# Hidden rows of an FP4 feed-forward layer as three tiles of columns, and the last ten token tiles turned on TensorE

## The chip, the cores and the metric

The kernel runs on one core of one Trainium2 chip. The metric is the device time of one execution in microseconds; a median over runs is given. A second number, the span, is the time from the first to the last instruction in one profiled execution.

## The reference

A transformer layer over 8 sequences of 1024 tokens with 512 features, all in float32. First latent attention on the normalised input, then a feed-forward block whose weights and activations are rounded to a 4-bit grid in blocks of 16, each with a residual:

```python
x = x + attn(layernorm(x))               # 16 heads of 32 + 16 rotary columns, latent 128, causal
x = x + ffn(layernorm(x))

def fp4_quant_dequant(x):                # blocks of 16 along the last dimension
    scale = max(abs(xb)) / 6, at least 1e-12
    return nearest(GRID, abs(xb / scale)) * sign(xb) * scale     # GRID 0 .5 1 1.5 2 3 4 6

def ffn(x):                              # 512 -> 1408 -> 512
    gate = q(x) @ q(w_gate).T
    up   = q(x) @ q(w_up).T
    h    = silu(gate) * up
    return q(h) @ q(w_down).T
```

Here `q` is `fp4_quant_dequant`. What matters below is that a row of `h`, 1408 values of one token, is quantised along the row, and then has to stand with its 1408 values along the partitions, because TensorE sums over partitions. A tile of 128 tokens by 1408 columns has to be turned between the up and the down product.

## The kernel before

The 8192 tokens are 64 token tiles of 128 rows, numbered n; four of them, 512 tokens, form a unit, and a sequence is two units. A unit's attention is made of score steps: scores on TensorE, exponentials on ScalarE (L612), the clip and the sums on VectorE (L627, L656) and GpSimd (L630, L634), then the product with the values. A first unit of a sequence has 3 steps for each of four groups of heads, a second unit 7. The output projection (`out_proj`, L770) of a unit runs early in the next one; `fetch_wo` (L764) loads its weights again each time, and the result is stored to DRAM as `mid`, from which the feed-forward part reads it again as `y` and, for the residual, as `xr`.

The feed-forward work of earlier units is cut into pieces (`ffn_pieces`, L904) and laid between the score steps of later ones as fillers, so that TensorE has work while exponentials are computed. For token tile n the order is: `gate(n, 0..2)`, then `down(n - 2)`, then `up(n, 0..2)`; columns 0 to 511, 512 to 1023 and 1024 to 1407 are the three parts k (`FCH`, L31). Between them, `begin(n + 1)` puts the normalisation and quantisation of the next y in the VectorE order, `turned(n + 1)` turns it on TensorE, and `fetch(n + 2)` loads the one after it.

- `gate` multiplies and ScalarE copies the sum out of PSUM into the row tile `h` (L836, recorded at L142). `h` has two buffers, so the row of tile n uses the memory of tile n - 2, and the copy has to wait until that row has been moved away.
- `up` multiplies and VectorE forms the product with the gate in place (L851). After the last part the whole row of 1408 is put in VectorE's list: one maximum for the whole row (L261), the scales (L266 to L271), then for each part six passes that round it (L288, L296, L299, L302 twice, L284) and a transposition of its 32 x 32 blocks (L311).
- When all three parts are turned, `hidden_turned` (L862) sends 16 DMAs (`move_blocks`, L229, the issue is at L237) that carry the blocks to their places in `hT`. There is one buffer of `hT`; the move of tile n is sent after `down(n - 1)` has used its own. Each DMA carries 32 partitions with 11 runs of 32 values.
- `down` waits for the move, and TensorE runs the product of 11 chunks into one PSUM bank; VectorE adds the residual (L899), and the store to `out` is sent (L902).
- The last token tile alone (`BY_PE`, L250) is turned on TensorE inside `down`: 11 transposes by the identity (`turn`, L215) into PSUM, and ScalarE copies them into `hT`.

Three PSUM banks (`bank`, L212) serve all products except scores and values, in turn: a product can start when the bank of the third last one has been read.

The order on TensorE, VectorE and ScalarE is written out by the program itself while it is built. A class `Clock` keeps an estimated time for each of the three. `slack` and `quantize` put VectorE jobs with estimated costs into two queues; `on_dve` fills the time up to a job's estimated readiness with jobs from the queues (`fill`); `need(key)` lays all jobs up to a key at once, before the piece that needs them. DMAs that wait for a moment (`send`, `pass_on`, `sent_by_now`) are put in SyncE's queue when TensorE's estimated time passes that moment or when something asks for them. All loads, stores and moves of the main part go through that one queue of SyncE, which works in order: an issue that waits holds all behind it. `MOVE` (L249) is the estimated time of a move.

The moves of the normalised x of the attention part (`xnT`, also 16 DMAs for 256 rows of tokens, twice per unit) use the same function and the same queue.

In the first four units, in place of feed-forward pieces, `weight_pieces` (L322) loads the feed-forward weights in chunks, quantises them with the same jobs and turns them on TensorE; the chunks lie in the two buffers of `h` and that of `hT`.

Of the kernel before, what the change touches and what calls it, by code (L numbers as in the profile page):

```python
# [42 lines left out]
def tile_mla_then_fp4_ffn(  # L43
# [149 lines left out]
    pair = p1.tile([P, 2, D], F32, tag="xp", name="xp_0_0")  # L193
    for t in range(2):
        nc.sync.dma_start(out=pair[:, t, :], in_=x[0, t * P : (t + 1) * P, :])
    other = p1.tile([P, NFC, P], F32, tag="hT", name="x_0").rearrange("p n k -> p (n k)")
    for t in range(2):
        nc.sync.dma_start(out=other[:, t * D : (t + 1) * D], in_=x[0, (2 + t) * P : (3 + t) * P, :])
    first_x = [pair[:, t, :] for t in range(2)] + [other[:, t * D : (t + 1) * D] for t in range(2)]
    nc.scalar.dma_start(out=wdkv, in_=w_dkv.rearrange("(c p) n -> p c n", p=P))  # L200
    nc.scalar.dma_start(out=wdq, in_=w_dq.rearrange("(c p) n -> p c n", p=P))
    nc.scalar.dma_start(out=wkr, in_=w_kr.rearrange("(c p) n -> p c n", p=P)[:, :, 32:64])
# [43 lines left out]
        clk.sent_by_now(key)  # L246
        clk.pe = max(clk.pe, arrive.pop(key))

    MOVE = 9.0  # L249
    BY_PE = (4 * 2 * B - 1,)  # L250


    def quantize_jobs(q, width, key, scales_in):

        nb = width // BLK
        q3 = q.rearrange("p (b k) -> p b k", k=BLK)
        got, jobs = {}, []

        def amax():
            got["sc"], got["rs"] = sc, rs = scales_in()  # L260
            nc.vector.tensor_reduce(rs, q3, AX.X, ALU.max, apply_absolute_value=True)  # L261

        def scales():
            sc, rs = got["sc"], got["rs"]

            nc.vector.tensor_scalar(sc, rs, 1.0 / 6.0, None, ALU.mult)  # L266
            nc.vector.scalar_tensor_tensor(rs, sc, -4.0, rs, ALU.mult, ALU.add)
            nc.vector.scalar_tensor_tensor(rs, sc, -2.0, rs, ALU.mult, ALU.add)
            nc.vector.scalar_tensor_tensor(sc, rs, 1.0 / 6.0, sc, ALU.mult, ALU.add)
            nc.vector.tensor_scalar(sc, sc, 1e-12, None, ALU.max)  # L270
            nc.vector.reciprocal(rs, sc)  # L271

        jobs.append((0.06 + 0.0011 * width, amax, key, True))
        jobs.append((1.1 + 0.008 * nb, scales, key, True))
        for o in range(0, width, 512):
            step = min(512, width - o)
            part, bl = q[:, o : o + step], slice(o // BLK, (o + step) // BLK)
            nbl = step // BLK
            part3 = part.rearrange("p (b k) -> p b k", k=BLK)

            def times(which, part3=part3, bl=bl, nbl=nbl):
                by = got[which][:, bl].unsqueeze(2).to_broadcast([P, nbl, BLK])
                if which == "sc":
                    nc.vector.tensor_tensor(part3, part3, by, ALU.mult)  # L284
                else:


                    nc.vector.scalar_tensor_tensor(  # L288
                        part3, part3, BELOW_ONE, by, ALU.mult, ALU.mult
                    )  # L290

            def steps(part=part, step=step):
                got["m"] = m = p1.tile([P, 512], F32, tag="m", name="m")[:, :step]
                nc.vector.tensor_scalar(  # L296
                    m.bitcast(U32), part.bitcast(U32), EXP_MASK, None, ALU.bitwise_and
                )
                nc.vector.tensor_scalar(m, m, 1.0, MAGIC, ALU.max, ALU.mult)  # L299

            def to_grid(op, part=part):
                nc.vector.tensor_tensor(part, part, got["m"], op)  # L302

            pass_cost = 0.06 + 0.00125 * step
            jobs.append((pass_cost, lambda f=times: f("rs"), key, True))
            jobs.append((1.2 * pass_cost, steps, key, True))
            jobs.append((pass_cost, lambda f=to_grid: f(ALU.add), key, False))
            jobs.append((pass_cost, lambda f=to_grid: f(ALU.subtract), key, False))
            jobs.append((pass_cost, lambda f=times: f("sc"), key, True))
            if key[0] == "h" and key[1] not in BY_PE:  # L310
                jobs.append((0.72, lambda p=part: nc.vector.transpose(p, p), key, True))  # L311
        return jobs

    def quantize(q, width, key):
        def own():
            return [p1.tile([P, 88], F32, tag=x, name=x)[:, : width // BLK] for x in ("sc", "rs")]

        for cost, run, k, free in quantize_jobs(q, width, key, own):
            clk.later.append((cost, run, k, 0.0, free))


    def weight_pieces():  # L322
# [4 lines left out]
            chunks.append([(w_gate[rows, :], wg_T[:, :, rows]), (w_up[rows, :], wu_T[:, :, rows])])  # L327
        for c in range(NDC):
            rows = slice(c * P, (c + 1) * P)
            chunks.append([(w_down[rows, :], wd_T[:, :, rows])])  # L330
        raws = {}

        def load(i):

            if i % 3 < 2:
                raw = p2.tile([P, FF], F32, tag="h", name="wraw")
            else:
                raw = p1.tile([P, NFC, P], F32, tag="hT", name="wraw_hT")
                raw = raw.rearrange("p n k -> p (n k)")
            raws[i], at = raw, 0  # L340
            for src, _ in chunks[i]:
                nc.sync.dma_start(out=raw[:, at : at + src.shape[1]], in_=src)
                at += src.shape[1]
            quantize(raw[:, :at], at, ("w", i))

        def piece(i, at, dst, off, n):
            if i == 0 and at == 0:
                for k in range(3):
                    load(k)
            clk.need(("w", i))  # L350
            turn(raws[i][:, at : at + n * P], dst[:, off : off + n], n)
            if at + n * P == sum(src.shape[1] for src, _ in chunks[i]):
                raws.pop(i)
                if i + 3 < len(chunks):
                    load(i + 3)

        pieces = []
        for i, parts in enumerate(chunks):
            at = 0
            for src, dst in parts:  # L360
                for off, width in FCH if src.shape[1] == FF else [(0, D)]:
                    n = width // P
                    pieces.append((i, at, dst, off // P if src.shape[1] == FF else 0, n))
                    at += width
        return [(0.5, lambda x=x: piece(*x)) for x in pieces]


# [435 lines left out]
    def begin(n):  # L803
# [1 line left out]
        yTs[n] = yT = p2.tile([P, NDC, P], F32, tag="yT", name="yT")  # L805
        jobs = normed(ys[n], ("y", n))
        scales_in = lambda: (yT[:, 0, : D // BLK], yT[:, 1, : D // BLK])
        jobs += [x[:3] for x in quantize_jobs(ys[n], D, ("y", n), scales_in)]
        ahead_of_rows(jobs)

    def hidden(n, w, off, width):
# [9 lines left out]
        return pg  # L821

    def turned(n):
        clk.need(("y", n))
        clk.pe = max(clk.pe, clk.dve)
        yT = yTs.pop(n)
        turn(ys[n], yT, NDC)
        ys[n] = yT

    def gate(n, k):  # L830
        if k == 0:
            clk.need(("h", n - 2))
            clk.sent_by_now(("h", n - 2))
            hs[n] = p2.tile([P, FF], F32, tag="h", name="h")
        off, width = FCH[k]
        copy_out(hs[n][:, off : off + width], hidden(n, wg_T, off, width))  # L836
        if k == 2:
            silus.append(
                lambda: on_act(4.0, lambda: nc.scalar.activation(hs[n], hs[n], AF.Silu))
            )  # L840

    def up(n, k):
        while silus:
            silus.popleft()()
        off, width = FCH[k]
        h = hs[n][:, off : off + width]
        pg = hidden(n, wu_T, off, width)
        on_dve(
            0.1 + 0.00115 * width,
# [2 lines left out]
        )  # L852
        if k == 2:
            ys.pop(n)
            quantize(hs[n], FF, ("h", n))
            slack(0.0, lambda: hidden_turned(n), ("h", n))

    hTs = {}

    waits, used = {}, set()  # L860

    def hidden_turned(n, done=None):  # L862

        if n in BY_PE:
            return
        if n > 0 and n - 1 not in used:
            waits[n] = clk.dve
            return
        h = hs.pop(n)

        def make():
            hTs[n] = p1.tile([P, NFC, P], F32, tag="hT", name="hT")
            return hTs[n]

        move_blocks(h, make, ("h", n), clk.dve if n == 0 or done is None else max(done, clk.pe))

    def down(n):
        clk.need(("h", n))
        clk.sent_by_now("store")
        ends[n] = p3.tile([P, D], F32, tag="xo", name=f"xr_{n}")  # L880
        nc.sync.dma_start(out=ends[n], in_=mids.pop(tiles[n]))
        if n in BY_PE:
            hTs[n] = p1.tile([P, NFC, P], F32, tag="hT", name="hT")
            for off, width in FCH:
                f0, c = off // P, width // P
                turn(hs[n][:, off : off + width], hTs[n][:, f0 : f0 + c, :], c)
            hs.pop(n)
        else:
            arrived(("h", n))
        hT = hTs[n]  # L890
        pd = bank("pd")
        for i in range(NFC):
            mm(pd, lhsT=hT[:, i, :], rhs=wd_T[:, i, :], start=(i == 0), stop=(i == NFC - 1))
        hTs.pop(n)
        used.add(n)
        if n + 1 in waits:
            hidden_turned(n + 1, waits.pop(n + 1))
        xt = ends.pop(n)
        on_dve(0.7, clk.pe + 0.3, lambda: nc.vector.tensor_tensor(xt, pd, xt, ALU.add))  # L899
        u, t = tiles[n]  # L900
# [161 lines left out]
```

## Time and profile before

| what | value |
|---|---|
| median of three runs | 3772.24 us (3765.41 to 3773.14) |
| the profiled execution | 3769.9 us |
| its span | 3768.2 us |
| TensorE's granted clock, mean | 0.976 |
| TensorE busy | 3550.3 us (94%) |
| VectorE busy | 2852.6 us (76%) |
| ScalarE busy | 1136.8 us (30%) |
| GpSimd busy | 669.8 us (18%) |
| DMAs for hT, xnT on SyncE's queue | 1008, 480 |

An engine is busy while one of its instructions runs; the rest of the span it is idle, and a list of waits names what ended each idle time. "ACT h L142 <- DMA hT<-h" reads: ScalarE, about to write `h` at line 142, was idle until the DMA that moves `h` into `hT` had landed. Tile names leave buffer numbers out. A timeline line gives the start in us from the span's beginning, the length, the engine, the line, the operation, the tiles written and read with their shapes, and how many were merged in the line. A row of stretches gives, for each, its length, the busy time and number of instructions of TensorE, its weight loads, VectorE, ScalarE and GpSimd, then the granted clock, the share of the DMA engines and GB/s. An issue on SyncE's queue is a sequencer's work, not counted as busy; its length is the time that the queue was taken by it.

### The profile page before, as it was taken

The numbers are of one execution on the slowest core, as the hardware profiler recorded it, in microseconds if no ns is written. First come the engines' busy times: TensorE is split into PE (matmuls) and PEld (weight loads), VectorE is DVE, ScalarE is ACT, GpSimd is POOL, SyncE is SP. The second block draws the span as 40 slices with busy tenths as digits, with TensorE's granted clock in tenths as the row PEclk, the third lists the DMA queues.
The fourth block names the chain that finished last, engine by engine and source line by source line (L and its number), as shares of the span: only waits on it lengthen the run. The fifth ranks groups of instructions, "written<-read, shape, count | busy, mean of one in ns | idle before, by whom it ended". The sixth has DMA issues, their size and how long they took to land.

```text
span 3768.2 us, 45975 instructions
## 1 busy us (share of the span) xinstructions
PE 3550.3 (94%) x17119; PEld 1550.3 (41%) x17119; DVE 2852.6 (76%) x5024; ACT 1136.8 (30%) x1473; POOL 669.8 (18%) x838
## 2 busy tenths in 40 slices
PE   6997989999999999999999999999999999998998
PEld 3333334443444444444444444444443444443343
DVE  4886856787868778877888687887877886777876
ACT  2443442332223233223233332233323322332210
POOL 1333331111111111211111111112111111111100
PEclk9998999999999999999999999999999999999999
DMA  3212211222122211223121222212122112211122
GB/s 83 70 35 70 72 34 45 55 50 44 33 69 44 74 40 37 47 62 76 34 44 33 67 50 66 44 33 72 43 68 44 33 33 75 52 39 33 42 63 39
DMA packets 577038, 192.47 MB, mean 51 GB/s; under 512 B 514864, under 2 KB 515888, under 8 KB 576816
## 3 DMA queue, kind: packets, MB, share of 16 engines
q1 hardware_dynamic: 568512, 187.36, 21.1%
q10 hardware_dynamic: 8304, 2.18, 0.3%
q8 instruction: 136, 2.23, 0.2%
q14 instruction: 86, 0.70, 0.1%
HBM read 94.72 MB, written 33.55 MB: 34 GB/s over the span
## 4 chain that ended last, share of the span: by engine, by line
PE 58%; DVE 14%; SPq 6%; issue 3%; DMA 2%; ACT 2%; POOL 1%; DVEq 0%; ACTq 0%; POOLq 0%
PE pg L129 21%; PE pd L129 11%; PE sc_ps L129 8%; SPq L237 6%; PE po L129 5%; PE num L129 4%; PE pp L129 2%; DVE h L302 2%; DVE pT L656 2%; PE den L129 1%; DVE h L311 1%; DVE h L284 1%; DMA hT<-h 1%; PE pv L129 1%; PE pqr L129 1%
## 5 line engine op out<-in xcount | busy, mean ns | idle before, releaser
L612 ACT ACTIVATE pT<-sc_ps 128x1024 f32<-128x1024 f32 (+1 forms) x640 | 567.3, 940 | 1137.4 <-PE sc_ps L129 1020.0
L129 PE MATMUL pg<-wg_T,yT 128*128 128x512 f32 (+1 forms) x1536 | 641.7, 569 | 2.4 <-ACT h L142 1.7
L129 PE MATMUL pg<-wu_T,yT 128*128 128x512 f32 (+1 forms) x1536 | 638.9, 562 | 0.0
L129 PE MATMUL pd<-wd_T,hT 128*128 128x512 f32 x1408 | 620.8, 597 | 8.1 <-ACT h L142 5.3
L630 POOL TENSOR_SCALAR pT<-pT 128x1024 f32<-128x1024 f32 (+1 forms) x320 | 351.3, 1098 | 1049.1 <-ACT pT L612 677.4
L634 POOL TENSOR_SCALAR_AFFINE_SELECT pT<-pT 128x256 f32<-128x256 f32 (+1 forms) x384 | 238.9, 622 | 1587.9 <-DVE pT L627 1410.2
L656 DVE TENSOR_TENSOR pT<-pT 128x1024 f32<-128x1024 f32 (+3 forms) x528 | 463.7, 904 | 3.7 <-POOL pT L634 0.6
L627 DVE TENSOR_SCALAR pT<-pT 128x1024 f32<-128x1024 f32 (+1 forms) x320 | 206.2, 644 | 327.7 <-ACT pT L612 326.9
L129 PEld LDWEIGHTS pg<-wg_T,yT 128*128 128x128 f32 x1536 | 294.4, 194 | 337.4 <-issue 256.0
L129 PEld LDWEIGHTS pg<-wu_T,yT 128*128 128x128 f32 x1536 | 282.6, 190 | 315.7 <-issue 248.7
L129 PEld LDWEIGHTS pd<-wd_T,hT 128*128 128x128 f32 x1408 | 265.0, 190 | 349.7 <-issue 327.2
L129 PE MATMUL sc_ps<-qc,kT 32*128 32x512 f32 (+3 forms) x3072 | 342.4, 530 | 25.0 <-ACT pT L612 24.9
L142 ACT COPY h<-pg 128x512 f32<-128x512 f32 (+1 forms) x192 | 102.4, 554 | 786.5 <-DMA hT<-h 415.0
L129 PE MATMUL num<-pT,v 128*32 128x512 f32 (+3 forms) x3072 | 327.8, 499 | 11.8 <-POOL pT L634 11.2
L129 PE MATMUL sc_ps<-qr,kr 32*128 32x512 f32 (+3 forms) x3072 | 309.2, 487 | 4.2 <-DVE qr L548 4.2
L129 PE MATMUL po<-wo,aT 128*128 128x512 f32 x512 | 236.5, 622 | 36.6 <-DMA wo<-in_w_o_dram 24.5
L302 DVE TENSOR_TENSOR h<-h,m 128x512 f32<-128x512 f32 (+1 forms) x384 | 260.1, 677 | 10.7
L851 DVE TENSOR_TENSOR h<-pg,h 128x512 f32<-128x512 f32 (+1 forms) x192 | 122.6, 639 | 127.9 <-PE pg L129 124.3
L129 PEld LDWEIGHTS sc_ps<-qc,kT 32*128 32x128 f32 x3072 | 115.5, 185 | 242.1 <-issue 149.8
L129 PEld LDWEIGHTS sc_ps<-qr,kr 32*128 32x128 f32 x3072 | 146.8, 188 | 109.7 <-issue 84.2
L129 PEld LDWEIGHTS po<-wo,aT 128*128 128x128 f32 x512 | 101.5, 200 | 169.2 <-issue 121.8
L129 PEld LDWEIGHTS num<-pT,v 128*32 128x32 f32 x3072 | 67.9, 108 | 224.8 <-issue 132.3
(109 smaller groups left out, 3412.7 us busy)
## 6 DMA issues: line engine op xcount, KB each, us to landing
hT<-h SPq DMA_DIRECT2D x1008, 44.0 KB, 2.1
xo<-in_x_dram SPq DMA_DIRECT2D x64, 256.0 KB, 2.7
wo<-in_w_o_dram SPq DMA_DIRECT2D x16, 1024.0 KB, 5.2
mid<-xo SPq DMA_DIRECT2D x64, 256.0 KB, 2.2
y<-mid SPq DMA_DIRECT2D x64, 256.0 KB, 2.8
xr<-mid SPq DMA_DIRECT2D x64, 256.0 KB, 2.7
out_dram<-xr SPq DMA_DIRECT2D x64, 256.0 KB, 2.0
xp<-in_x_dram SPq DMA_DIRECT2D x30, 512.0 KB, 3.9
```

The source lines that it names most:

```text
L129: nc.tensor.matmul(dst, **kw)
L142: on_act(0.1 + 0.0009 * src.free_size(), lambda: nc.scalar.copy(dst, src))
L237: nc.sync.dma_start(out=dst[32 * q : 32 * q + 32, :, 32 * g : 32 * g + 32], in_=src4[32 * g : 32 * g + 32, q],)
L284: nc.vector.tensor_tensor(part3, part3, by, ALU.mult)
L302: nc.vector.tensor_tensor(part, part, got["m"], op)
L311: jobs.append((0.72, lambda p=part: nc.vector.transpose(p, p), key, True))
L612: lambda: nc.scalar.activation(part, sc[:, 2 * k : 2 * k + 2, :cols], AF.Exp, scale=SM_SCALE),
L627: lambda: nc.vector.tensor_scalar(part, part, E_HI, E_LO, ALU.min, ALU.max),
L630: nc.gpsimd.tensor_scalar(part, part, E_HI, E_LO, ALU.min, ALU.max)
L634: nc.gpsimd.affine_select(out=diag, in_=diag, pattern=[[0, 2], [0, len(segs)], [1, P]], compare_op=ALU.is_ge, fill=0.0, base=0, channel_mu ...
L656: lambda a=whole, b=part: nc.vector.tensor_tensor(a, a, b, ALU.add),
L851: lambda: nc.vector.tensor_tensor(h, pg, h, ALU.mult),
```

## The change

The row of a token tile is no longer one tile of 1408 columns but three (512, 512 and 384), with tags h0, h1, h2 and two buffers each; `hT` likewise becomes hT0, hT1, hT2 with one buffer each. What follows from that in the code:

- `quantize_jobs` takes a list of parts. The maximum is one reduction per part; the scales are still computed once for the row. The jobs of part k have the key (name, n, k), so that a piece can ask for one part.
- After the transposition of a part on VectorE, `row_turned(n, k)` sends the 16 DMAs of that part, or leaves it waiting until `down(n - 1)` has used its part k. A row is moved by 48 DMAs instead of 16, each with 4 or 3 runs of 32 values per partition instead of 11.
- `gate(n, k)` asks for part k of tile n - 2 instead of the whole row, and `down` waits for a part ahead of that part's matmuls.
- `BY_PE` holds the last ten token tiles, 54 to 63. Their rows are not turned on VectorE and not moved; `turn_here` turns part k on TensorE just ahead of `gate(n + 2, k)`, or inside `down` for the last two.
- Silu runs once for each part, one after the other. The weights are loaded, quantised and turned in such parts too, and w_down comes in three DMAs per chunk.
- `MOVE` is 8.0 instead of 9.0, and some estimated costs of the planner differ.

```diff
-    MOVE = 9.0
-    BY_PE = (4 * 2 * B - 1,)
+    MOVE = 8.0
+    BY_PE = range(4 * 2 * B - 10, 4 * 2 * B)
...
-        def amax():
-            got["sc"], got["rs"] = sc, rs = scales_in()
-            nc.vector.tensor_reduce(rs, q3, AX.X, ALU.max, apply_absolute_value=True)
+        def amax(part, at):
+            if at == 0:
+                got["sc"], got["rs"] = scales_in()
+            nc.vector.tensor_reduce(
+                got["rs"][:, at : at + part.shape[1] // BLK],
+                part.rearrange("p (b k) -> p b k", k=BLK),
...
-            if key[0] == "h" and key[1] not in BY_PE:
-                jobs.append((0.72, lambda p=part: nc.vector.transpose(p, p), key, True))
+            if then is not None:
+                jobs.append((1.0 * cost, lambda p=part, k=k: then(p, k), name, True))
...
     def gate(n, k):
-        if k == 0:
-            clk.need(("h", n - 2))
-            clk.sent_by_now(("h", n - 2))
-            hs[n] = p2.tile([P, FF], F32, tag="h", name="h")
         off, width = FCH[k]
-        copy_out(hs[n][:, off : off + width], hidden(n, wg_T, off, width))
+        if n > 1:
+            clk.need(("h", n - 2, k))
+            if n - 2 in BY_PE:
+                turn_here(n - 2, k)
+            clk.sent_by_now(("h", n - 2, k))
+        hs[n, k] = p2.tile([P, width], F32, tag=f"h{k}", name=f"h{k}")
+        copy_out(hs[n, k], hidden(n, wg_T, off, width))
...
+    def row_turned(n, k, done=None):
+
+        if done is None:
+            done = clk.dve
+        if n > 0 and (n - 1, k) not in used:
+            waiting[n, k] = done
+            return
+        h = hs.pop((n, k))
+
+        def make():
+            hTs[n, k] = p1.tile([P, FCH[k][1] // P, P], F32, tag=f"hT{k}", name="hT")
+            return hTs[n, k]
+
+        move_blocks(h, make, ("h", n, k), max(done, clk.pe if (n, k) in waiting else done))
+
+    def turn_here(n, k):
+        width = FCH[k][1]
+        clk.pe = max(clk.pe, clk.dve)
+        hTs[n, k] = p1.tile([P, width // P, P], F32, tag=f"hT{k}", name="hT")
+        turn(hs.pop((n, k)), hTs[n, k], width // P)
...
     def down(n):
-        clk.need(("h", n))
...
+        for k, (off, width) in enumerate(FCH):
+            if n in BY_PE:
+                if (n, k) not in hTs:
+                    clk.need(("h", n, k))
+                    turn_here(n, k)
+            else:
+                arrived(("h", n, k))
+            for i in range(off // P, (off + width) // P):
+                mm(
+                    pd,
+                    lhsT=hTs[n, k][:, i - off // P, :],
...
+            hTs.pop((n, k))
+            used.add((n, k))
+            if (n + 1, k) in waiting:
+                row_turned(n + 1, k, waiting[n + 1, k])
+                waiting.pop((n + 1, k))
```

## The prediction

> **What bounds the kernel now.** The page's busy row comes first: no other engine is near TensorE. Lines marked L are the kernel's; PE is TensorE, ACT ScalarE, DVE VectorE, SPq the queue of SyncE.
>
> ```profile
> span 3768.2 us, 45975 instructions
> PE 3550.3 (94%) x17119; PEld 1550.3 (41%) x17119; DVE 2852.6 (76%) x5024; ACT 1136.8 (30%) x1473; POOL 669.8 (18%) x838
> ```
>
> So the change can win only what is left of TensorE's idle 218 us, and lose by lengthening it. The list of waits says who the idle time is for; a row gives the total in us, how often, and the longest.
>
> ```profile
> ACT h L142 <- DMA hT<-h: 415.0, 31, 25.9
> PE pqr L129 <- ACT h L142: 41.9, 5, 9.0
> PE pp L129 <- ACT h L142: 13.5, 5, 3.1
> DVE ny L376 <- DMA y<-mid: 38.5, 16, 4.8
> ```
>
> ScalarE's copy of a new gate row waits 31 times until the row two tiles earlier, which has the same buffer, has been moved. Mostly that is hidden; ten times TensorE then waits for a PSUM bank. The timeline around one of the five long ones (start, length, engine, and in brackets the idle time before it):
>
> ```profile
> 1366.43 1.06 PE L129 MATMUL num<-pT,v 128*32 128x512 f32 x8
> 1375.82 2.08 PE L129 MATMUL pqr<-cq,wqr 128*128 128x512 f32 x2 [8.32 <-ACT h L142]
> ...
> 1375.18 0.59 ACT L142 COPY h<-pg 128x512 f32<-128x512 f32 x1 [17.82 <-DMA hT<-h]
> ...
> 1362.98 10.51 SPq L237 DMA_DIRECT2D hT<-h  x16
> ```
>
> The move is 16 issues in a row on SyncE's queue, 10.5 us, and lands 1.4 us later; only then may the copy write. Cut into stretches from tile 15's gate on, the profile repeats every 10 tiles, with some 18 us of TensorE idle in each:
>
> ```profile
> 1359.00:1868.00 509.00, 491.20 (x2213) 215.59 (x2212) 397.76 (x703) 152.43 (x194) 85.36 (x106) 0.98 0.22 51
> 1868.00:2377.00 509.00, 489.23 (x2201) 214.54 (x2200) 394.51 (x699) 151.07 (x191) 83.06 (x104) 0.98 0.22 50
> ```
>
> **What the change can win.** A part of a row is moved when VectorE has turned it, and a gate copy waits for its own part alone. Tile 14's parts are turned by 1341.7, 1357.3 and 1362.9. Its first move can run 1341.7 to 1352.2, so the copy at 1362.7 need not wait, and the 8.32 us go. The same holds for the second idle stretch of the period, 2.59 us ahead of a pp matmul at 1470.0 (tile 16's parts are turned by 1438.6, 1452.0, 1457.0; copies at 1461 and 1465). After a gap TensorE also runs slower for a while: behind the long one the pqr pair takes 2.08 us instead of 1.12 and the next 16 gate matmuls 7.86 instead of 7.03, together 1.8; behind the short one the pp group takes 3.56 instead of 1.99, 1.6. The Trainium skill (TensorE: Matmul & The Clock Gate, "HAM oscillation — how this bites in real kernels") asks only that there be no idle gap above about 3.4 us; by that the short gap would cost nothing after itself, and the sum would be 5 x 1.6 = 8 us less gain. I take the row. Per period 8.3 + 1.8 + 2.6 + 1.6 = 14.3; five periods: 71.5. In the start-up of this stretch one gap of 1.7 (662.8) goes: 2.
>
> At the end (from 3333): gaps of 2.05, 0.81, 7.77 and 6.69, behind copies that waited 15 to 18.5 us for moves, 17.3, and about 5 of slow clock: 22. From 3600 on, five gaps ahead of down matmuls (1.16, 1.56, 1.99, 0.57, 2.86): 8. The last tile's second product starts with the part that is ready instead of after all three: the last matmuls now end at 3763.8; turning part by part they end about 5 earlier.
>
> The price there: nine more tiles are turned on TensorE, 99 transposes. Those of y are 256 in 39.3 us, so 0.153 each: 15, all of it on the bounding engine. Taken away with it: 9 x (0.71 + 0.71 + 0.57) = 18 us of VectorE's transposes and 144 DMAs. The 27 copies out of PSUM (0.59) fall to ScalarE, 30% busy. If that cover fails they cost 16. The maximum as three reductions costs VectorE 2 x 0.685 + about 0.53 against 1.61, 0.3 a tile, 19 in all, which balances the 18; three Silu calls for one cost ScalarE some 0.3 a tile. The weight loads keep their pace: each is turned 512 columns at a time as before. Sum of the gains: 71.5 + 2 + 22 + 8 + 5 - 15 = 93.
>
> **What it costs on SyncE's queue.** A move of a part is still 16 DMAs, so 54 tiles issue 48 each instead of 16: 2592 for 1008. Does a DMA of 128 pieces (4 column blocks) cost less to issue than one of 352 (11)? The trace has two sizes, 352 pieces for hT and 256 for xnT; the columns are least/median/most ns.
>
> ```profile
> L237 SPq DMA_DIRECT2D hT<-h x1008: 585/616/1884, 651.0 to 3735.1; - x168
> ...
> L237 SPq DMA_DIRECT2D xnT<-xp x480: 585/609/1823, 70.3 to 3199.7; - x160
> ```
>
> Same floor, medians 7 ns apart: the price is per DMA. With the 44 ns between, 16 take 10.5 us, three parts 31.5, of a mean 50.9 us per tile. The Trainium skill speaks against such a price: DMA: Bandwidth & Descriptors, "Anatomy of one DMA — SWDGE (gpsimd) path", puts sequencer dispatch at about 50 ns and most of the 2 us in the landing. With that, 48 DMAs would hold the queue for 2.4 us and nothing below would be late. But that section tells of GpSimd's path, and the row is this queue: I take 0.6. Ends: 0.24 a DMA if it fell with the pieces (a part 3.8 us, no loss), 0.66 if not.
>
> The queue is in order, and what stands behind a row's moves now comes up to 21 us later, less the time between its first and last part (5 to 25). Two things stand there.
>
> First, **the output projection's weights**. Once in a period:
>
> ```profile
> 1579.57 10.50 SPq L237 DMA_DIRECT2D hT<-h  x16
> 1590.12 0.60 SPq L189 DMA_DIRECT2D xo<-in_x_dram  x1
> 1590.84 0.39 SPq L768 DMA_DIRECT2D wo<-in_w_o_dram  x1
> ...
> 1596.71 15.37 PE L129 MATMUL po<-wo,aT 128*128 128x512 f32 x32 [3.57 <-DVE h L851]
> ```
>
> wo lands at 1596.6 and po starts at 1596.7: no slack. Tile 19's parts are turned at 1570.9, 1575.3 and 1579.4; three moves from 1570.9 end at 1602.4, wo is issued near 1603, 12.4 later. At the five such places I get 11.2, 12.4, 11.9, 12.4 and 11.3: 59 us, straight onto TensorE, whose matmuls behind po (scores too) wait with it.
>
> Second, **y and xo**, which VectorE reads in order. At 1319.19 y is issued right behind tile 13's move (parts turned 1297.7, 1302.6, 1308.5). Three moves from 1297.7 end at 1329.2, y lands 2.9 after its issue, at 1332.6; its statistics (L376) stand at 1323.4: VectorE waits 9 us, and behind L376 wait the clips, the up products and the bank releases. VectorE is busy 397 of 509 us, so some is absorbed. I pushed each lateness down VectorE's order, let its idle gaps eat it, and took as a TensorE stall what exceeds the distance from an instruction's end to the matmul that needs it (median 9.4 us for the clips, 5.0 for the up products' banks, 4.4 for the down sums). The 20 y loads that stand directly behind a move: 76 us of stalls; xo: 19; all y loads, if the parts overtake those too: 160, with xo 180. Floor 0: a VectorE delay could be made up wholly. I take 76 + 19 = 95, since only those 20 are sure to be behind.
>
> Other effects: the part that a copy waits for is now the third. By the same queue arithmetic third copies wait 5.5, 7.5 and some 8.3 us three times a period, just before the 9.7 us of down matmuls that hide them: 0. xnT has 12 us of slack or more when it follows one part: 0, up to 7 a period if it follows two.
>
> **Sum.** The profiled run took 3769.9 us (span 3768.2), inside the three runs shown (median 3772.2). 3769.9 - 93 + 59 + 95 = 3831; I say 3830, 1.5% slower.
>
> **Rivals.** (1) *The queue's delay is absorbed on VectorE.* For it: 22% idle. Only wo bites: 3770 - 93 + 59 = 3736, faster. (2) *Small DMAs are cheaper to issue.* Against it, the equal floors. It decides the sign: at about 9 us a part the same pushing gives 50 instead of 180, and wo about 40; then the sum is 3740 to 3770, and below 7 us a part near 3680. (3) *All y loads are late*, VectorE becomes the bound in the odd blocks: 3770 - 93 + 59 + 180 = 3916. (4) *The parts don't come early*: a part's jobs are forced only at its own gate, behind the next y's jobs (about 7 us), so moves start late and copies still wait. For it: half of the tiles are finished within 5 us of their gate now. Gains fall to 30, losses too, near 3800. (5) Gains and losses cancel, 3763 to 3777.
>
> **How the numbers follow.** Forecast 0.43 (its own range 3785 to 3880); (1) 0.17; (2) 0.12; (3) 0.12; (4) 0.09; (5) 0.07. Faster is (1) and (2), 0.29; within 0.2%, about what a measurement can tell, 0.07; slower the rest, 0.64. The range leaves out the cheapest half of (2), and the worst part of (3): 3690 to 3915.
>
> **What would show it.** Right: hT issues of 2592 at 585 ns or more, SPq near 55% busy; the ACT wait for hT well below 415 us and the pqr gap gone; waits of po for wo grown by 11 to 12 us in five places; the y wait above 38.5 us, many times over. Wrong: issues near 300 ns; wo overtaking the moves because the planner sends parts later; y waits that stay small; or stalls of TensorE on turned parts after tile 54.

## The result, and the profile after

| what | before | after |
|---|---|---|
| median | 3771.01 us | 4149.17 us (4146.40 to 4150.56) |
| span of the profiled execution | 3768.2 us | 4148.5 us |
| TensorE busy, idle | 3550, 218 us | 3654, 495 us |
| mean granted clock | 0.976 | 0.944 |
| gaps of TensorE over 1.5 us | 41, together 177 us | 71, together 437 us |

The changed kernel is slower by 10.0%: ratio 1.1004, 95% interval 1.0985 to 1.1023. The forecast was 1.5%. Of the 380 us more in the span, 277 are idle time of TensorE. The other 103 are longer busy time: 15 for the 99 transposes, by the 0.153 us of the prediction, and 88 left over, at a lower clock: the granted clock stood at 0.50 for 184 us of the run before and for 471 us of this one.

The head of the page after the change:

```profile
span 4148.5 us, 49052 instructions
...
PE 3653.5 (88%) x17218; PEld 1584.8 (38%) x17218; DVE 2848.9 (69%) x5144; ACT 1168.4 (28%) x1628; POOL 662.1 (16%) x838
```

VectorE has as many busy microseconds as before (2848.9 against 2852.6), so no work was added to it that could matter. It waits more. The list of waits of the changed kernel (total us, times, longest), the first two over all engines, the rest TensorE's own:

```profile
DVE ny L386 <- DMA y<-mid: 470.0, 47, 23.1
...
ACT h L142 <- DMA hT<-h: 240.8, 46, 11.9
...
PE pg L129 <- DVE xr L931: 129.8, 20, 8.8
PE po L129 <- DMA wo<-in_w_o_dram: 90.0, 7, 15.9
PE num L129 <- DVE pT L637: 64.4, 24, 8.2
PE num L129 <- POOL pT L644: 59.6, 33, 6.2
PE pv L129 <- DVE xr L931: 36.1, 5, 7.7
```

The wait that was to be shortened, ScalarE's for the move, fell from 415.0 to 240.8 us and from 25.9 at the longest to 11.9. The rows of TensorE waiting for that copy (41.9 and 13.5 us before) are gone from its list. In their place VectorE's wait for y rose from 38.5 us in 16 places to 470.0 in 47. TensorE pays for it at many places: a product that waits for a bank which VectorE's residual sum (L931) has yet to read, and values that wait for clipped exponentials (L637, and L644 on GpSimd behind it).

One such case shows the whole path. SyncE's queue, then VectorE, then TensorE, each a timeline of the changed kernel (start, length, engine, line, operation, idle time ahead of it in brackets):

```profile
1973.40 10.24 SPq L237 DMA_DIRECT2D hT<-h  x16
...
1984.39 21.18 SPq L237 DMA_DIRECT2D hT<-h  x32
2005.67 0.53 SPq L811 DMA_DIRECT2D y<-mid  x1
```

```profile
1995.99 0.69 DVE L311 TENSOR_TENSOR h<-h,m 128x512 f32<-128x512 f32 x1
2008.50 0.69 DVE L386 BATCH_NORM_STATS2 ny<-y 128x6 f32<-128x512 f32 x1 [11.82 <-DMA y<-mid]
...
2024.04 0.71 DVE L876 STREAM_TRANSPOSE h<-h 128x512 f32<-128x512 f32 x1
...
2026.38 0.68 DVE L931 TENSOR_TENSOR xr<-pd,xr 128x512 f32<-128x512 f32 x1
```

```profile
2018.97 1.99 PE L129 MATMUL pp<-xnT,wdkv 128*128 128x256 f32 x8
2027.12 9.37 PE L129 MATMUL pg<-wu_T,yT 128*128 128x512 f32 x16 [6.15 <-DVE xr L931]
```

The load of y stands behind two parts of a move, 32 issues. It goes out at 2005.67 and has landed by 2008.5. VectorE stands at its statistics for 11.82 us, and behind them in its order stand the sum that frees a bank and the rest of the row that it had begun to round. TensorE idles 6.15 us for the bank and then runs its 16 matmuls in 9.37 instead of 7.03, with the granted clock at 0.50 up to 2031.66. The row's first part is turned only at 2024.04, so its own move starts late as well. Such lateness could feed on itself, if the next y stood behind that move. Here it does not: the next y goes out at 2041.80, when its buffer has just become free. But the head of SyncE's queue does wait longer for a transposed part than it did; the kernel before, then the changed one:

```profile
SPq L237 <- DVE h L311: 218.8, 55, 12.2
```

```profile
SPq L237 <- DVE h L876: 623.9, 42, 31.3
```

While the head of the queue waits for VectorE, all loads behind it wait too. Nearly all of the 623.9 us are waits for the first part of a row, 42 of them, 15 us in the mean: the queue has come to the move long before VectorE has turned the part. How much of the rise comes of late loads of y is seen in the first experiment below. From the end of the transposes that free y's buffer to the issue of the next y, over tiles 3 to 53, the mean was 2.5 us before and is 13.2 now (medians 0.6 and 13.5). Of these 51 loads 43 went out more than 1 us late, where 21 did before, and 36 more than 10 us late, where none did. Those that directly follow an hT move rose from 15 to 31. Ten tiles took 509 us; now they take 587. From tile 54 on, where no rows are moved, this vanishes. Stretches of 50 us (length; busy time and count of TensorE, its loads, VectorE, ScalarE, GpSimd; clock, DMA share, GB/s), one from the main part and one from the end:

```profile
1700.00:1750.00 50.00, 35.45 (x149) 15.77 (x142) 16.88 (x31) 9.02 (x13) 7.71 (x10) 0.86 0.40 108
...
4000.00:4050.00 50.00, 50.00 (x141) 24.29 (x140) 41.27 (x87) 9.13 (x18) 1.09 (x2) 1.00 0.05 16
```

Without moves TensorE has no gap in these 50 us and runs at full clock. The stretch of the main part has one of the five long waits for wo, 14.55 us at a mean clock of 0.86, and is worse than most: from tile 0's gate to tile 54's, 394 of 3154 us are idle, where the kernel before has 101 of 2756.

### The profile page after: what moved, and what is told of

Same layout as the page of the kernel before. It is cut to its first block, busy times and chain, and to the rows that moved or that the text cites. A ratio compares the mean times of both kernels' runs of the same rounds, so it can differ in the third digit from the quotient of the medians.

```text
span 4148.5 us, 49052 instructions
## 1 busy us (share of the span) xinstructions
PE 3653.5 (88%) x17218; PEld 1584.8 (38%) x17218; DVE 2848.9 (69%) x5144; ACT 1168.4 (28%) x1628; POOL 662.1 (16%) x838
## 5 line engine op out<-in xcount | busy, mean ns | idle before, releaser
L622 ACT ACTIVATE pT<-sc_ps 128x1024 f32<-128x1024 f32 (+1 forms) x640 | 566.1, 937 | 1237.5 <-PE sc_ps L129 1140.4
L129 PE MATMUL pg<-wu_T,yT 128*128 128x512 f32 (+1 forms) x1536 | 686.6, 596 | 131.2 <-DVE xr L931 129.8
L129 PE MATMUL pd<-wd_T,hT 128*128 128x512 f32 x1408 | 631.1, 603 | 15.4 <-DMA hT<-h 11.5
L644 POOL TENSOR_SCALAR_AFFINE_SELECT pT<-pT 128x256 f32<-128x256 f32 (+1 forms) x384 | 239.2, 623 | 1625.4 <-DVE pT L637 1264.3
L129 PEld LDWEIGHTS pg<-wu_T,yT 128*128 128x128 f32 x1536 | 298.1, 202 | 482.4 <-issue 268.7
L640 POOL TENSOR_SCALAR pT<-pT 128x1024 f32<-128x1024 f32 (+1 forms) x320 | 342.0, 1069 | 844.8 <-ACT pT L622 586.9
L666 DVE TENSOR_TENSOR pT<-pT 128x1024 f32<-128x1024 f32 (+3 forms) x528 | 472.4, 919 | 3.0
L129 PE MATMUL num<-pT,v 128*32 128x512 f32 (+3 forms) x3072 | 351.7, 511 | 125.5 <-DVE pT L637 64.4
L386 DVE BATCH_NORM_STATS2 ny<-y 128x6 f32<-128x512 f32 x64 | 44.3, 692 | 470.0 <-DMA y<-mid 470.0
L637 DVE TENSOR_SCALAR pT<-pT 128x1024 f32<-128x1024 f32 (+1 forms) x320 | 206.9, 646 | 181.0 <-ACT pT L622 180.4
L311 DVE TENSOR_TENSOR h<-h,m 128x512 f32<-128x512 f32 (+1 forms) x384 | 261.9, 682 | 10.5
L797 DVE TENSOR_TENSOR xo<-po,xo 128x512 f32<-128x512 f32 x64 | 43.9, 687 | 242.4 <-PE po L129 141.9
```

The source lines that it names most:

```text
L129: nc.tensor.matmul(dst, **kw)
L386: nc.vector.bn_stats(st, xt)
L622: lambda: nc.scalar.activation(part, sc[:, 2 * k : 2 * k + 2, :cols], AF.Exp, scale=SM_SCALE),
L637: lambda: nc.vector.tensor_scalar(part, part, E_HI, E_LO, ALU.min, ALU.max),
L640: nc.gpsimd.tensor_scalar(part, part, E_HI, E_LO, ALU.min, ALU.max)
L644: nc.gpsimd.affine_select(out=diag, in_=diag, pattern=[[0, 2], [0, len(segs)], [1, P]], compare_op=ALU.is_ge, fill=0.0, base=0, channel_mu ...
```

## The experiments

The theory: the time that 48 issues take on SyncE's queue makes y, xo and wo late, VectorE with them, and TensorE with VectorE. Against it stand three rivals: that parts and the new order of VectorE's jobs cost the time; that the turns on TensorE do; that a queue taken for so long does no harm, whatever stands in it.

### y on another queue

```diff
     def fetch(n):
...
-        nc.sync.dma_start(out=ys[n], in_=mids[tiles[n]])
+        nc.scalar.dma_start(out=ys[n], in_=mids[tiles[n]])
```

> The changed kernel, with the load of y issued from ScalarE's queue instead of SyncE's, at the same place of the program. Theory (the moves hold SyncE's queue, y comes late, VectorE stands at its statistics and TensorE waits for banks and clips behind it): the wait of VectorE for y falls from 470 us to under 60, the waits of the up matmuls for the down sum (129.8 us) nearly vanish, and with the slow clock behind those gaps about 300 us go: 3850 us (3790 to 3920). Rival (the planner's finer keys put VectorE's jobs in a worse order and the y wait only shows where it stands): 4050 us or more, with the same up matmuls waiting.

Measured: 3931.04 us, ratio to before 1.0423 (1.0408 to 1.0439): 218 us less than the changed kernel, from one line, and 11 above the upper end that the theory gave. Its waits:

```profile
DVE ny L386 <- DMA y<-mid: 62.9, 29, 9.1
...
PE pg L129 <- DVE xr L931: 53.5, 10, 6.0
...
ACT pT L622 <- DMA hT<-h: 198.2, 22, 15.0
```

VectorE's wait for y fell from 470.0 to 62.9 us and TensorE's for the bank from 129.8 to 53.5. That late y loads are the largest single cause found is shown. It isn't a clean removal: the last row is new. y's issue waits on ScalarE's queue up to 14 to 17 us, until a move has landed, and ScalarE's exponentials (L622) wait behind it; the issue comes 8.5 us after the buffer is free in the mean. The trace's semaphores tell why. Each DMA reports its landing by a semaphore. All DMAs of SyncE and ScalarE in this program use eight of them in turn, and most issues first wait until the last DMA with the same semaphore has landed. Of the 51 y loads of tiles 3 to 53, 41 went out more than 1 us late, each within 0.3 us of such a landing, 36 times that of an hT move's DMA. So this wait is the program's doing, and y was taken from behind the issues of a move but not from behind its landing. The 218 us include that price, and what y costs is probably more.

The wait at the head of SyncE's queue for a turned part is still 476.0 us here, in 47 places. So of its rise from 218.8 to 623.9 at most about 148 us can come of late loads of y; the larger part comes with moves in parts wherever y is loaded.

### The output projection's weights on a third queue as well

```diff
-        nc.sync.dma_start(out=outs["wo"], in_=w_o.rearrange("(c p) n -> p c n", p=P))
+        nc.gpsimd.dma_start(out=outs["wo"], in_=w_o.rearrange("(c p) n -> p c n", p=P))
...
-        nc.sync.dma_start(out=ys[n], in_=mids[tiles[n]])
+        nc.scalar.dma_start(out=ys[n], in_=mids[tiles[n]])
```

> As the run with y on ScalarE's queue, and the load of the output projection's weights issued from GpSimd. Theory: the five long waits of the output projection (14 to 16 us each) go back to some 4 us, 50 us and 10 of slow clock less than with y alone: about 3790 us. Rival (a load of 1 MB is late because the DMA engines are busy with small pieces, not because of the queue): no change against y alone.

Measured: 3891.80 us, 1.0314 (1.0296 to 1.0331), 39 less than with y alone. TensorE's wait for wo, with y alone and then with both moved:

```profile
PE po L129 <- DMA wo<-in_w_o_dram: 93.5, 8, 16.4
```

```profile
PE po L129 <- DMA wo<-in_w_o_dram: 29.8, 7, 11.0
```

GpSimd's loads have eight semaphores of their own, so wo isn't tied to a move's landing as y is. The wo part is real, but 119 us above the kernel before remain, where about 20 were expected. xo, still on SyncE's queue, keeps VectorE waiting for 110.1 us in 12 places, and ScalarE waits for moves before its copies as before.

### No moves at all: every tile turned on TensorE

```diff
-    BY_PE = range(4 * 2 * B - 10, 4 * 2 * B)
+    BY_PE = range(4 * 2 * B)
```

> The changed kernel with all 64 token tiles turned on TensorE: no row of h is moved or transposed on VectorE, all else as changed. Theory (moves are the whole loss): TensorE gets 54 x 11 x 0.153 = 91 us more work than in the changed kernel, the 380 us of loss and the old waits for moves go: about 3790 us (3730 to 3850), y waits under 60 us. Rival (the planner's order): over 4000 us.

Measured: 3692.78 us, 0.9788 (0.9773 to 0.9803): the fastest of all, 456 us under the changed kernel and 2.1% under the one before, in spite of 594 more transposes (about 91 us at 0.153).

```profile
span 3690.4 us, 45758 instructions
...
PE 3581.4 (97%) x17812; PEld 1600.7 (43%) x17812; DVE 2726.9 (74%) x4982; ACT 1246.7 (34%) x1790; POOL 654.9 (18%) x838
```

The parts, their order and their costs in the planner are still there but for the transposes on VectorE, so the first rival falls. It is 97 us faster than was expected, and below the whole range given. Against the kernel before, TensorE's idle time falls from 218 to 109 us. It is busy 3581 us, of which some 106 are transposes of rows beyond those of before, at 0.153; the other 3475 compare with its 3550, at a clock of 0.992 instead of 0.976. VectorE has 122 us less to do than in the changed kernel, since it transposes no rows, so the gain over the kernel before isn't that of the moves alone.

### The kernel before, with 48 DMAs per row

```diff
+            cuts = ((0, 4), (4, 8), (8, 11)) if key[0] == "h" else ((0, 8),)
...
-                    nc.sync.dma_start(
-                        out=dst[32 * q : 32 * q + 32, :, 32 * g : 32 * g + 32],
-                        in_=src4[32 * g : 32 * g + 32, q],
-                    )
+                    for a, b in cuts:
+                        nc.sync.dma_start(
+                            out=dst[32 * q : 32 * q + 32, a:b, 32 * g : 32 * g + 32],
+                            in_=src4[32 * g : 32 * g + 32, q, a:b],
+                        )
```

> The kernel before, unchanged in its order, with each of the 16 DMAs of a row's move cut in three by columns: 48 DMAs, all sent when the whole row is turned. Theory (the number of DMAs alone does it): a move holds the queue for 31.5 us instead of 10.5, y and wo stand behind it, and gate copies wait 21 us longer as well: 4150 to 4450 us. Rival (the order of the changed kernel is what costs): 3770 to 3850 us.

Measured: 4459.93 us, 1.1822 (1.1804 to 1.1839).

```profile
ACT h L142 <- DMA hT<-h: 1026.8, 55, 39.5
...
DVE ny L378 <- DMA y<-mid: 343.5, 33, 23.0
```

The number of DMAs alone, with rows, buffers and order as before, costs 687 us. Small DMAs are not cheaper to issue: 599 ns in the median here, 616 in the kernel before. The next run has parts and, like this one, turns only the last tile on TensorE; it is 246 us faster. So parts that are moved when they are turned do win time, but less than their issues cost.

### One tile on TensorE instead of ten; ten in the kernel before

In the changed kernel:

```diff
-    BY_PE = range(4 * 2 * B - 10, 4 * 2 * B)
+    BY_PE = (4 * 2 * B - 1,)
```

> The changed kernel, but only the very last token tile turned on TensorE, as before the change: the other part of the change alone. Theory (the queue is the bound where rows are moved in parts): the nine tiles 54 to 62 lose what the others lose, 7 to 8 us each, and at the very end, where no attention lies between, a tile takes the queue's 31 to 34 us instead of 30: 4149 + 60 to 100, about 4225 us. Rival (turning on TensorE only adds its 15 us): 4135 us.

Measured: 4213.83 us, 1.1185 (1.1168 to 1.1201), 65 more than the changed kernel. Its waits:

```profile
DVE ny L386 <- DMA y<-mid: 516.3, 51, 22.8
...
PE pd L129 <- DMA hT<-h: 54.9, 15, 7.4
```

In the kernel before, with rows still in one tile:

```diff
-    BY_PE = (4 * 2 * B - 1,)
+    BY_PE = range(4 * 2 * B - 10, 4 * 2 * B)
...
+    def turn_row(n):
+        clk.pe = max(clk.pe, clk.dve)
+        hTs[n] = p1.tile([P, NFC, P], F32, tag="hT", name="hT")
+        for off, width in FCH:
+            f0, c = off // P, width // P
+            turn(hs[n][:, off : off + width], hTs[n][:, f0 : f0 + c, :], c)
+        hs.pop(n)
...
+            if n - 2 in BY_PE:
+                turn_row(n - 2)
```

> The kernel before, rows in one tile, with the last ten token tiles turned on TensorE: that part of the change alone. Theory (from the sum: gaps at the end that go, 30 us, against 15 us of transposes; the last row isn't overlapped by parts): 3750 to 3757 us. Rival (the end is bound by VectorE, and TensorE's transposes come on top): 3785 us.

Measured: 3743.73 us, 0.9925 (0.9911 to 0.9940). The row of TensorE waiting for ScalarE's copy in front of pqr is untouched by it, since it belongs to the main part:

```profile
PE pqr L129 <- ACT h L142: 41.7, 5, 8.8
```

So the turns on TensorE are a gain by themselves, 28 us in the kernel before (the prediction's terms for the end make 20; the run is 6 us beyond the fastest that was expected) and 65 among the longer queue's delays. The second rival falls.

### All tiles on TensorE, rows in one tile

The same `turn_row` in the kernel before, for all 64 tiles:

```diff
-    BY_PE = (4 * 2 * B - 1,)
+    BY_PE = range(4 * 2 * B)
...
+            if n > 1:
+                turn_row(n - 2)
```

> The kernel before, rows in one tile, with all 64 token tiles turned on TensorE just ahead of the gate that needs their buffer. Theory (what makes the all-on-TensorE kernel fast is that no row is moved; parts matter little then): within 25 us of 3693. Rival (parts are worth it by themselves: the first gate need not wait for the last part on VectorE): TensorE waits at each row's last part for VectorE, 2 to 5 us at half of the tiles, 3770 us or more.

Measured: 3713.21 us, 0.9853 (0.9838 to 0.9868). Cutting the rows in three, without moves, is worth 20 us (3713 against 3693). What the change costs is in the moves.

### Every second tile on TensorE

```diff
-    BY_PE = range(4 * 2 * B - 10, 4 * 2 * B)
+    BY_PE = [n for n in range(4 * 2 * B) if n % 2 or n >= 4 * 2 * B - 10]
```

> The changed kernel, with every odd token tile and the last ten turned on TensorE, so that every second row is moved in parts. Theory: the queue is held for 31.5 us in 100 instead of in 51, but in bursts as long as before, so what stands right behind a burst is still late. Against all 64 on TensorE (3693) it spares 27 x 1.7 = 46 us of TensorE and keeps up to half of the loss that moved rows still show, 547 us over that without them: between 3650, if slack swallows single bursts, and 3900; I expect 3780. Rival (each move costs TensorE nothing when it is alone): 3647.

Measured: 3965.36 us, 1.0526 (1.0508 to 1.0543): 185 us above what was expected. Half the moves should have left the queue ample time. Counted from the kernel without moves, and with the 45 us of transposes that 27 moved tiles save, a moved tile costs (3965.4 - 3692.8 + 45.4) / 27 = 11.8 us here; in the changed kernel it is (4149 - 3693 + 91) / 54 = 10.1.

```profile
DVE ny L386 <- DMA y<-mid: 245.7, 24, 21.8
DVE xo L797 <- DMA xo<-in_x_dram: 159.0, 12, 23.9
```

```profile
SPq L237 <- DVE h L876: 556.8, 21, 30.3
PE pr L129 <- DMA xnT<-xp: 71.9, 5, 15.0
```

The loss doesn't come from the queue's mean load. Each burst costs for itself, by what stands behind it: y waits about as often per moved tile (24 times for 27) and as long as with all moves. The head of the queue waits for VectorE longer at a time than with all moves, 26.5 us in the mean, and in 20 of these 21 places it has sent off a y just before. The largest wait of TensorE here is that for xnT: in all five places 14 of its 16 DMAs stand behind two parts of a row.

### The queue held, with nobody waiting

On top of the kernel without moves, 16 DMAs after each part's turn copy pieces of hT into DRAM where nobody reads them:

```diff
+        junk = dram.tile([4, 4, 32, width // P, 32], F32, tag=f"junk{k}", name="junk")
+        src = hTs[n, k]
+
+        def hold():
+            for g in range(4):
+                for q in range(4):
+                    nc.sync.dma_start(
+                        out=junk[g, q],
+                        in_=src[32 * q : 32 * q + 32, :, 32 * g : 32 * g + 32],
+                    )
+
+        clk.send(clk.pe, hold, ("junk", n, k))
```

> All 64 token tiles turned on TensorE, and after each part is turned 16 DMAs of the same shape as a part's move, from the turned part to a scratch tensor in DRAM that nothing reads: SyncE's queue is held for some 31 us per tile, but nobody waits for what is carried, and the buffer is not written again for a tile's time. Theory (holding the queue is by itself most of the loss; y, xo, xnT and the output projection's weights are late behind it): 3850 to 4050 us, with a wait of VectorE for y of 150 us or more. Rival (the loss comes from waiting for the moved parts: copies and down products): 3690 to 3720 us.

Measured: 3800.80 us, 1.0074 (1.0057 to 1.0091), 108 more than without the holds and 49 below the low end of what the theory expected. More than half of the 108 lie at the end: from tile 54's gate on the kernel takes 483 us instead of 425; 24 of these 58 us come after the last matmul, where the last store to `out` stands behind 48 holds. Up to tile 54 the holds cost 51 us, under 1 a tile. A hold and the y behind it on SyncE's queue, then two waits of this kernel:

```profile
2004.90 31.41 SPq L910 DMA_DIRECT2D junk<-hT  x48
...
2041.86 0.32 SPq L811 DMA_DIRECT2D y<-mid  x1
```

```profile
DVE ny L386 <- DMA y<-mid: 31.5, 14, 7.7
```

```profile
PE po L129 <- DMA wo<-in_w_o_dram: 63.9, 13, 14.3
```

The queue is taken for as long per tile as in the changed kernel, for 64 tiles instead of 54, and it isn't harmless: wo is late. But y hardly is (its issue comes 0.8 us after its buffer is free), because these issues wait for no work of VectorE, only for ScalarE's copies of the turned parts (304.1 us, 65 times), come in a block behind the gate pieces and are over when y is due. So the third rival falls, and the theory in the form "the queue's time is what costs" falls with it. What is left, argued from the two traces and not isolated in a run, is where the burst lies: the moves wait at the head for VectorE, and so end just when the loads that VectorE needs are due. Two more things differ in this run and were not separated: VectorE transposes no rows, and nothing waits for what the holds carry.

## Why the prediction was wrong, step by step

- **The bound.** That TensorE sets the end, and that the change can win only its idle time, held: with no moves at all TensorE is 97% busy.
- **The gains.** That gate copies would find their part moved was right: the 41.9 and 13.5 us rows of TensorE are gone. What that was worth in the main part was not measured apart. The end from tile 54's gate on took 450.5 us and takes 434.1, 16 less; the terms of the prediction for it (22 + 8 + 5 - 15) make 20.
- **The price of an issue.** 0.6 us per DMA whatever its size was right: 2592 issues of at least 585 ns, median 599, and 16 of a whole row took 10.5 us, 16 of a part 10.2. The queue was taken by issues for 2062 us, 50% of the span, where 55% was forecast. Had the prediction taken the 50 ns that the Trainium skill (DMA: Bandwidth & Descriptors, "Anatomy of one DMA — SWDGE (gpsimd) path") gives for GpSimd's path, nothing would have been late in it; the kernel before with 48 DMAs, 18% slower, shows which of the two counts here.
- **wo.** Forecast 59 us at five places. The gaps there were 4.27, 3.57, 4.20, 3.26 and 4.32 us and are 15.89, 14.55, 14.14, 14.46 and 14.50: 54 more, 9.9 to 11.6 each. Right.
- **y and xo: the step that failed.** "The 20 y loads that stand directly behind a move ... I take 76 + 19 = 95, since only those 20 are sure to be behind." In the run 43 of the 51 y loads of the main part went out late, 36 of them by more than 10 us; VectorE waits for y 47 times, 10 us in the mean, 470 in all, and xo adds 99.3 in 12 places. Moving y alone to another queue gave back 218 us. If the other terms of the sum stand, y and xo with their clock cost 380 + 93 - 59 = 414 us instead of 95.
- **Why it failed.** The working kept the order of the old queue, in which 20 y loads stand directly behind a move; with moves in parts nearly all y loads were late, which was its upper end. And it charged no clock behind the new gaps. Split by the prediction's own terms, the 414 are some 305 us of gaps and 110 of slow clock, an estimate: 277 of idle time more, and 87 of gaps that were to go, less 59 for wo; 88 of busy time beside the transposes, and 22 of slow clock that was to go. Moving y alone gave back 160 us of idle time and 59 of busy time, and 160 is what the working had for all y loads late. Some 125 us of gaps beyond its upper end of 180 are not explained. The pushing took the times at which parts are turned from the trace of before, so a late y could not delay the turning of a row, its move and the next y. The single links of such a loop are in the trace, but that it closes isn't shown: in the case above the next y is on time, and the wait at the head of the queue stays at 476.0 us without y on it.
- **A term left out.** The working credited the slow clock behind every gap that goes, 1.6 to 1.8 us each, and charged none behind the gaps that come. TensorE's busy time grew by 88 us beside the transposes, with the granted clock at 0.50 for 471 us instead of 184.
- **The rivals.** The delay is not absorbed, small DMAs are not cheaper, parts come early. Nearest was the third, all y loads late, with 3916; it had the late loads right, and lacked the clock and those 125 us of gaps.

What stays open is how the cost divides. With y and wo on other queues 3892 us are left, 199 above the kernel without moves, and of these xo, the copies of ScalarE that still wait for a move, and ScalarE's own issues were not separated. The holds gave 108 us and the alternating tiles 318 over their transposes, and no single price per burst explains both. A second buffer for y, so that it could be loaded a tile earlier, wasn't tried.

## What to carry to other kernels

Cutting a transfer in parts so that it starts earlier multiplies its issues, and on an in-order queue these can be paid by whatever stands behind, even where the queue is half empty in the mean. How much is paid depends on where the burst lies: 48 issues a tile cost under 1 us up to tile 54 in the run with holds, which wait for no work of VectorE, and some 10 in the changed kernel, whose moves do. When you forecast such a change, list every load on the queue with the instruction that reads it, and work out anew which of them will stand behind a burst, instead of taking the old order and the old times. Charge each new gap of TensorE with the slow clock behind it. Here the cure was to have no moves: 693 transposes more on the bounding engine than before, about 106 us, and still 2.1% faster.

## What was unexpected of the hardware

- On SyncE's queue an issue of a DMA within SBUF in three-dimensional pieces takes 585 ns at least and about 0.6 in the median whether it carries 96, 128 or 352 pieces, and copies into DRAM of the parts' shape take 549 and 598. A plain load such as y or wo takes 0.32 to 0.39 us there on its own.
- A load put on ScalarE's queue still waited for moves issued by SyncE, up to 14 to 17 us, and showed it as a wait of ScalarE. That is not the queues' doing: this program's DMAs of both queues share eight completion semaphores, and 41 of 51 issues waited for the one that they would use. wo on GpSimd's queue had others.
- A gap costs TensorE more than its length. Behind 6.15 us of idle time the granted clock was 0.50 up to 2031.66, and 16 matmuls took 9.37 instead of 7.03 us; behind 2.59 us in the kernel before it was 0.50 from 1469.82 to 1473.23; over the whole run 260 us more in gaps came with 88 us more of busy time, and the kernel without moves, 109 us idle in all, ran at a clock of 0.992.
